# A four-layer graph network on one core: projections moved into layer 0's second pass over adj, and the sorting of rows moved beside layer 1's relayout

## The chip, the core and the metric

The kernel runs on one core of one Trainium2 chip. The metric is the device time in microseconds of one execution; lower is better. The kernel before takes 3336.72 us (median of three executions, 3329.15 to 3339.13).

## The reference

Four layers over N = 2708 nodes of 128 features, all with the same adjacency matrix `adj` (2708 x 2708, fp32, about five non-zeros a row, among them the diagonal). Each layer adds to x what it makes of the normed rows h = max(layernorm(x), 0). Layers 0 and 1 and their hand-over are what the change touches:

```python
# layer 0
fc = h @ W + b
d = sum(adj, axis=1); s = 1 / (sqrt(d) + 1e-8)
x = x + (adj * s[:, None] * s[None, :]) @ fc
# layer 1: h again from the new x; Wq, Wk, Wv are 1024 x 128
q, k, v = ((h @ Wi.T).reshape(128, N, 8) for Wi in (Wq, Wk, Wv))
a = softmax(einsum('dnh,dmh->dnm', q, k) / sqrt(128) + 2 * adj, axis=2)
x = x + einsum('dnm,dmh->dnh', a, v).reshape(N, 1024) @ Wo.T
# layer 2: adj.T @ h / degree, two projections, batch norm, relu
# layer 3: sigmoid gates between neighbours, weighted by adj
```

Layer 1 has 128 "heads" d, of 2708 nodes and 8 features each. A head takes its nodes from the reshape, so the projections' result has to be written to DRAM and read back in another order. The kernel evaluates exp of the small logits by a polynomial and corrects the few neighbours of a node by themselves; for this it needs the list of each row's non-zeros (column and value, up to 16), and it works on the rows sorted by their number of neighbours.

## The kernel before

The rows are cut into 22 tiles of 128 (the last has 20). In layers 0 and 1 the order of instructions on each engine is the program's own (`tc.manual_schedule()`): nothing reorders them, and what should lie side by side is written side by side, by generators that are advanced step by step.

**Start (lines 254 to 350).** All of x is loaded; the three weights of layer 1 are loaded and turned (`by_head`); the first three tiles of adj are asked for. All 22 tiles are normed: statistics on VectorE (326, 327), root (329), scaling on VectorE (338), relu on ScalarE (342), transposes in groups of four (344) into `hT` (345). Then fc per tile, two matmuls, the second with one row for the bias (348, 349), and a copy (350).

**First load (386 to 417).** Each adj tile passes once, in an order that alternates between the `STAY` = 8 tiles that stay in SBUF, transposed, and the others. ScalarE sums the rows (393) and takes the root (397); VectorE finishes the scale factor (398, 399) and scales fc (400). For the ten tiles in `early` (0 to 7, 8 and 9) the search for neighbours is done too. Tiles that stay are transposed (`turned`, 303, copies 308), and products of staying tiles with fc tiles already scaled are issued a few at a time (`products`, 363). At the end `x` is updated for the eight (414).

**Search for neighbours (129 to 176).** Five generator steps per tile: the 8 largest of each of five segments (134); their places (138); the 16 largest of the 40 (144 to 148, with casts on GpSimd, 155 to 157); a one-hot of 16 x 40 on VectorE (160), multiplied by the columns on GpSimd (166); a sum over 40 on VectorE (174). `look(n)` advances it.

**Second load (493 to 522).** The other 14 tiles are loaded again (`rows_of_adj`, four buffers, asked for three tiles ahead), searched, transposed, tested for negative values on ScalarE (488, 506) and multiplied with all fc tiles (`product`, 469); `added` (476) updates x. When four tiles are done, their norm for layer 1 is queued and advanced two steps per tile (`norm`).

**Projections (620 to 655).** For each group of 512 rows (148 in the last) 24 matmuls (641), one per weight and head feature, six PSUM banks; each is written to one of 25 columns of `qkv`, by ScalarE and VectorE in turn (648, 650), so to a stride of 100 bytes; the group is stored to `qkv_c` (652). Between them `in_order` is advanced: it ranks the rows by number of neighbours (a prefix sum on VectorE) and scatters their lists into `list_d` with 22 indirect DMAs on GpSimd's queue (612).

**Layer 1 (686 to 1369).** `prepare` loads a group of four heads (`raw`, 548) and squares it (796). The main loop goes through 128 heads in six chunks each; GpSimd makes most of the keys' features and the value products two heads ahead (1150, `keys`, `with_values`). Beside it a chain of generators is advanced 1.5 steps per chunk: `by_node` (relayout of q, k, v from heads to nodes through DRAM, 195 steps), then `sorted_rows` (loads `list_d`), then `from_neighbours`.

Of the kernel before, what the change touches and what calls it, by code (L numbers as in the profile page):

```python
# [28 lines left out]
STAY = 8  # L29
# [16 lines left out]
def gnn4_kernel(  # L46
# [82 lines left out]
    def neighbours(t, sz, a, pool, seg0, at48):  # L129
# [41 lines left out]
        )  # L171
        yield
        col = pool.tile([P, KS], FP, name="n_col")
        nc.vector.reduce_sum(col[:sz], hot[:sz], axis=AX.X)
# [80 lines left out]
    pre = ExitStack()  # L255
    bp = pre.enter_context(tc.tile_pool(name="l01", bufs=1))
    hT = bp.tile([C, N], FP, name="hT")
    with ExitStack() as ph:
        lp = ph.enter_context(tc.tile_pool(name="l0", bufs=1))
        hp = ph.enter_context(tc.tile_pool(name="l0_h", bufs=3))  # L260
        np_ = ph.enter_context(tc.tile_pool(name="l0_n", bufs=2))
# [4 lines left out]
        pa = ph.enter_context(tc.tile_pool(name="l0_pa", bufs=1, space=PSUM))  # L266

        def by_head(src, name):

            nat = ap.tile([P, KC, C], FP, name=f"{name}_nat", tag="a_nat")  # L270
            nc.sync.dma_start(nat, src.rearrange("(t p) c -> p t c", p=P))
            dst = bp.tile([P, HEAD, C], FP, name=name)
            for i0, iw in _cuts(KC, 4):
                pt = ps.tile([P, BK], FP, name="w_ps", tag="tr")
                for i in range(iw):
                    nc.tensor.transpose(pt[:, i * P : (i + 1) * P], nat[:, i0 + i], ident)
                c0, cw = i0 * P // HEAD, iw * P // HEAD
                nc.vector.tensor_copy(
                    dst[:, :, c0 : c0 + cw],
                    pt[:, : iw * P].rearrange("p (c h) -> p h c", h=HEAD),  # L280
                )
            return dst
# [5 lines left out]
        def rows_of_adj(t):  # L288
            r0, sz = rows[t]
            a = ap.tile([P, N], FP, name="a_nat", tag="a_nat")  # L290
            nc.sync.dma_start(a[:sz], adj[r0 : r0 + sz])
            return a

        def turned(t, a, both):

            sz = rows[t][1]
            at = tp.tile([P, NT, P], FP, name="a_tr")
# [16 lines left out]
        fc = lp.tile([P, NT, C], FP, name="fc")  # L314
        junk = lp.tile([P, N], BF, name="junk")
        mv = lp.tile([P, NT, 2], FP, name="mv_0")
        nc.gpsimd.memset(mv, 1.0)
        with tc.manual_schedule():
            stay, gone = list(range(STAY)), list(range(STAY, NT))
            order = [t for two in zip(stay, gone) for t in two] + gone[STAY:]  # L320
            early = stay + gone[:2]
            wT = [by_head(w, f"wT{i}") for i, w in enumerate((wq, wk, wv))]
            nat = [rows_of_adj(t) for t in order[:3]]
            for t, (_, sz) in enumerate(rows):
                st = hp.tile([P, nc.vector.BN_STATS_DIM], FP, name="ln_st")
                nc.vector.bn_stats(st[:sz], x_sb[:sz, t])
                nc.vector.bn_aggr(mv[:sz, t], st[:sz])
            rstd = lp.tile([P, NT], FP, name="rstd_0")
            nc.scalar.activation(rstd, mv[:, :, 1], AF.Sqrt, bias=eps)
            nc.vector.reciprocal(rstd, rstd)  # L330
            for t0, tw in _cuts(NT, 4):
# [3 lines left out]
                for t in range(t0, t0 + tw):  # L335
                    sz = rows[t][1]
                    h = hp.tile([P, C], FP, name="h_0", bufs=4)
                    nc.vector.tensor_scalar(
                        h[:sz], x_sb[:sz, t], mv[:sz, t, 0:1], rstd[:sz, t : t + 1],
                        ALU.subtract, ALU.mult,  # L340
                    )
                    nc.scalar.activation(h[:sz], h[:sz], AF.Relu)
                    o = (t - t0) * P
                    nc.tensor.transpose(pt[:, o : o + sz], h[:sz], ident[:sz, :sz])
                nc.scalar.copy(hT[:, s0 : s0 + w], pt[:, :w])
            for t, (r0, sz) in enumerate(rows):
                pf = pm.tile([P, C], FP, name="fc_ps", tag="mm")
                nc.tensor.matmul(pf[:sz], hT[:, r0 : r0 + sz], w0_sb, start=True, stop=False)
                nc.tensor.matmul(pf[:sz], ones[0:1, :sz], b0_sb, start=False, stop=True)
                nc.scalar.copy(fc[:sz, t], pf[:sz])  # L350

            sums0 = [pa.tile([P, 4, C], FP, name=f"l0_s{g}") for g in range(-(-STAY // 4))]
# [18 lines left out]
            seg_i = lp.tile([P, SEG, 8], I32, name="seg_i")  # L371
            nc.gpsimd.iota(seg_i, pattern=[[seg_w, SEG], [0, 8]], base=0, channel_multiplier=0)
            seg0 = lp.tile([P, CAND], FP, name="seg0")
            nc.gpsimd.tensor_copy(seg0, seg_i.rearrange("p s e -> p (s e)"))
            at_i = lp.tile([P, CAND], I32, name="at_i")
            nc.gpsimd.iota(at_i, pattern=[[1, CAND]], base=0, channel_multiplier=0)
            at48 = lp.tile([P, CAND], FP, name="at48")
            nc.gpsimd.tensor_copy(at48, at_i)
            found = []

            def look(n):
                for _ in range(n):
                    while found and next(found[0], "done") == "done":
                        found.pop(0)

            seen = []
            for i, t in enumerate(order):
                r0, sz = rows[t]
                if i + 3 < NT:
                    nat.append(rows_of_adj(order[i + 3]))  # L390
                a = nat[i]
                look(3)
                nc.scalar.activation(
                    junk[:sz], a[:sz], AF.Copy, accum_out=deg[:sz, t : t + 1]
                )
                d = dinv[:sz, t : t + 1]
                nc.scalar.activation(d, deg[:sz, t : t + 1], AF.Sqrt)
                nc.vector.tensor_scalar_add(d, d, 1e-8)
                nc.vector.reciprocal(d, d)
                nc.vector.tensor_scalar_mul(fc[:sz, t], fc[:sz, t], d)  # L400
# [5 lines left out]
                products(8 if t in stay else 14)  # L406
                seen.append(t)
                ready += [(j, t) for j in sorted(there)]
                ready += [(t, m) for m in seen[:-1] if t in stay]
            look(6)  # L410
            nat = [rows_of_adj(t) for t in gone[:3]]
            products(len(ready))
# [6 lines left out]
            rs1 = lp.tile([P, NT], FP, name="rs1")  # L419
            normed = []  # L420

            def normed_rows(t0, tw):

                hg = hp.tile([P, 4, C], FP, name="h_1", bufs=2)
                for t in range(t0, t0 + tw):
                    sz = rows[t][1]
                    st = hp.tile([P, nc.vector.BN_STATS_DIM], FP, name="ln_st")
                    nc.vector.bn_stats(st[:sz], x_sb[:sz, t])
                    nc.vector.bn_aggr(mv[:sz, t], st[:sz])
                yield  # L430
                r = rs1[:, t0 : t0 + tw]
                nc.scalar.activation(r, mv[:, t0 : t0 + tw, 1], AF.Sqrt, bias=eps)
                yield
                nc.vector.reciprocal(r, r)
                for t in range(t0, t0 + tw):
                    sz = rows[t][1]
                    nc.vector.tensor_scalar(
                        hg[:sz, t - t0], x_sb[:sz, t], mv[:sz, t, 0:1], rs1[:sz, t : t + 1],
                        ALU.subtract, ALU.mult,
                    )  # L440
                for t in range(t0, t0 + tw):
                    sz = rows[t][1]
                    nc.scalar.activation(hg[:sz, t - t0], hg[:sz, t - t0], AF.Relu)
                yield
                pt = ps.tile([P, BK], FP, name="ln_ps", tag="tr")
                s0 = rows[t0][0]
                w = rows[t0 + tw - 1][0] + rows[t0 + tw - 1][1] - s0
                for t in range(t0, t0 + tw):
                    sz = rows[t][1]
                    o = (t - t0) * P  # L450
                    nc.tensor.transpose(pt[:, o : o + sz], hg[:sz, t - t0], ident[:sz, :sz])
                nc.scalar.copy(hT[:, s0 : s0 + w], pt[:, :w])
                yield

            def norm(n):
                for _ in range(n):
                    while normed and next(normed[0], "done") == "done":
                        normed.pop(0)

            groups = _cuts(NT, 4)  # L460
            while groups and sum(groups[0]) <= STAY:
                normed.append(normed_rows(*groups.pop(0)))
# [11 lines left out]
            def added(t, po):  # L474
# [5 lines left out]
                if groups and sum(groups[0]) == t + 1:  # L480
                    normed.append(normed_rows(*groups.pop(0)))
# [13 lines left out]
            for t in range(STAY, NT):  # L495
                if t + 3 < NT:
                    nat.append(rows_of_adj(t + 3))
                a = nat[t - STAY]
                sz = rows[t][1]
                if t not in early:  # L500
                    found.append(neighbours(t, sz, a, np_, seg0, at48))
                    look(2)
                there[t] = turned(t, a, False)
                if t - STAY + 1 < STAY:
# [4 lines left out]
                )  # L509
                if t > STAY:  # L510
                    pos[t - 1] = product(t - 1)
                if t - 2 in pos:
                    added(t - 2, pos.pop(t - 2))
                look(3)
                norm(2)
# [5 lines left out]
            while normed:  # L521
                norm(1)

    VW = HEAD + 1
    QKV = 3 * HEAD + 1
# [1244 lines left out]
```

## Time and profile before

| | us |
|---|---|
| median of three executions (3329.15 to 3339.13) | 3336.72 |
| the profiled execution, of its own | 3354.19 |
| its span | 3352.4 |
| start, norm, fc | 0 to 70 |
| first load | 70 to 211 |
| second load | 211 to 379 |
| projections, last matmul | 379 to 494 |
| last projections in DRAM | 511 |
| first square of layer 1 (796) | 540 |
| relayout's last copy | 931 |
| layer 1's last weighted moments (1210) | 2814 |

The profile names instructions by line, engine and operation, with the tiles that they write and read. A group's row gives its busy time, the mean of one instruction, and the idle time just before with what ended it. A table of stretches gives for each window its length, the busy time of PE (matmul), PEld (weight load), DVE (VectorE), ACT (ScalarE) and POOL (GpSimd) with the number of instructions, the granted TensorE clock, the share of the DMA engines and GB/s. A line of waits reads: engine, tile and line that waited, what it waited for, time in total, times, longest.

### The profile page before, as it was taken

The numbers are of one execution on the slowest core, as the hardware profiler recorded it, in microseconds if no ns is written. First come the engines' busy times: TensorE is split into PE (matmuls) and PEld (weight loads), VectorE is DVE, ScalarE is ACT, GpSimd is POOL, SyncE is SP. The second block draws the span as 40 slices with busy tenths as digits, with TensorE's granted clock in tenths as the row PEclk, the third lists the DMA queues.
The fourth block names the chain that finished last, engine by engine and source line by source line (L and its number), as shares of the span: only waits on it lengthen the run. The fifth ranks groups of instructions, "written<-read, shape, count | busy, mean of one in ns | idle before, by whom it ended". The sixth has DMA issues, their size and how long they took to land. (4 is left out here: it accounts for less than half of the span.)

```text
span 3352.4 us, 50866 instructions
## 1 busy us (share of the span) xinstructions
PE 2691.7 (80%) x17781; PEld 2273.0 (68%) x17781; DVE 2202.7 (66%) x5135; ACT 1314.8 (39%) x3127; POOL 2009.3 (60%) x2263
## 2 busy tenths in 40 slices
PE   6477884888789999999999999999888897796044
PEld 4476543777788887888888788877777886443033
DVE  3868753666678888888888788887666675213222
ACT  3485462555544444444444444444322232102010
POOL 0111115555588888888988888889656663000775
PEclk6688896999999999999999999999888999895565
DMA  3452274777743333333334333343465712541322
GB/s 113 175 227 93 76 326 128 208 214 206 211 131 114 125 125 127 128 132 128 119 138 139 126 141 125 137 143 121 94 148 143 166 48 64 193 176 56 106 83 61
DMA packets 312741, 462.08 MB, mean 138 GB/s; under 512 B 159650, under 2 KB 234404, under 8 KB 289330
## 3 DMA queue, kind: packets, MB, share of 16 engines
q1 hardware_dynamic: 280870, 289.79, 28.3%
q0 software_dynamic: 31600, 168.86, 14.7%
q8 instruction: 148, 2.42, 0.3%
q14 instruction: 123, 1.01, 0.1%
HBM read 344.89 MB, written 113.67 MB: 137 GB/s over the span
## 5 line engine op out<-in xcount | busy, mean ns | idle before, releaser
L1238 PE MATMUL g_ps<-mw,fT 128*128 128x128 f32 x5632 | 817.5, 287 | 155.2 <-ACT fT L1228 115.1
L1238 PEld LDWEIGHTS g_ps<-mw,fT 128*128 128x128 f32 x5632 | 715.4, 196 | 290.6 <-ACT fT L1228 178.4
L1228 ACT COPY fT<-f_ps 128x512 f32<-128x512 f32 (+1 forms) x768 | 420.6, 548 | 1216.7 <-PE f_ps L1226 1216.6
L1200 PE MATMUL m_ps<-y,fk 128*128 128x128 f32 (+1 forms) x5632 | 768.2, 280 | 0.0
L1200 PEld LDWEIGHTS m_ps<-y,fk 128*128 128x128 f32 (+1 forms) x5632 | 699.9, 194 | 15.4
L1150 POOL TENSOR_TENSOR y<-bk,raw 128x792 f32<-128x792 f32 x256 | 415.8, 1624 | 432.1 <-ACT y L1181 420.3
L1246 DVE TENSOR_TENSOR z<-g_ps,bq 128x324 f32<-128x324 f32 (+1 forms) x768 | 355.6, 463 | 435.0 <-PE g_ps L1238 433.6
L1226 PE MATMUL f_ps<-ident,fq 128*128 128x128 f32 x2816 | 441.6, 276 | 14.4 <-DVE v_sum L817 9.3
L1252 DVE TENSOR_REDUCE o_raw<-z 128x36 f32<-128x324 f32 (+1 forms) x768 | 355.8, 463 | 26.4
L1150 POOL TENSOR_TENSOR fk<-bk,raw 128x352 f32<-128x352 f32 (+1 forms) x384 | 357.7, 955 | 0.1
L1226 PEld LDWEIGHTS f_ps<-ident,fq 128*128 128x128 f32 x2816 | 340.2, 144 | 16.2 <-DVE v_sum L817 10.6
L1150 POOL TENSOR_TENSOR fk<-raw,bk 128x352 f32<-128x352 f32 (+1 forms) x512 | 312.6, 640 | 3.1 <-ACT bk L719 2.3
L1147 DVE TENSOR_TENSOR fq<-bq,kq_ps 128x528 f32<-128x528 f32 (+1 forms) x512 | 288.2, 605 | 0.0
L930 POOL TENSOR_TENSOR c_z<-c_kv,c_q 128x1024 f32<-128x1024 f32 (+1 forms) x121 | 284.2, 2349 | 2.2 <-DMA c_kv<-kv_n,srt 1.4
L971 PE MATMUL v_ps<-c_v,ident 128*128 128x512 f32 (+1 forms) x484 | 233.3, 605 | 15.3 <-ACT c_acc L986 15.3
L1591 POOL DMA_INDIRECT g<-gate_d,srt x121 | 120.4, 995 | 110.2 <-issue 109.0
L1147 DVE TENSOR_TENSOR fq<-kq_ps,bq 128x352 f32<-128x352 f32 (+1 forms) x512 | 171.9, 378 | 0.0
L155 POOL CAST n_fl<-n_ci 128x40 f32<-128x40 int32 (+1 forms) x22 | 4.8, 218 | 251.9 <-DVE n_ci L138 251.9
L936 DVE TENSOR_REDUCE c_c<-c_z 128x128 f32<-128x1024 f32 (+1 forms) x121 | 147.5, 1219 | 3.4 <-POOL c_z L930 3.2
L954 DVE TENSOR_TENSOR c_v<-c_kv,c_c 128x1024 f32<-128x1024 f32 (+1 forms) x121 | 146.7, 1212 | 0.0
L971 PEld LDWEIGHTS v_ps<-c_v,ident 128*128 128x128 f32 (+1 forms) x484 | 82.0, 189 | 79.1 <-issue 58.8
L915 POOL DMA_INDIRECT c_kv<-kv_n,srt x121 | 117.8, 974 | 23.1 <-issue 9.6
(290 smaller groups left out, 3714.1 us busy)
## 6 DMA issues: line engine op xcount, KB each, us to landing
a_nat<-in_adj_dram SPq DMA_DIRECT2D x34, 1354.0 KB
qkv_c<-qkv SPq DMA_DIRECT2D x5, 6400.0 KB
a<-in_adj_dram SPq DMA_DIRECT2D x21, 1354.0 KB
kv_n<-n_kv SPq DMA_DIRECT2D x16, 1344.0 KB
o_g<-o_raw SPq DMA_DIRECT2D x32, 396.0 KB
q_n<-n_q SPq DMA_DIRECT2D x16, 672.0 KB
o_cr<-o_c SPq DMA_DIRECT2D x21, 512.0 KB
r_raw<-o_g SPq DMA_DIRECT2D x22, 396.0 KB
```

What stands on the lines that cost most here:

```text
L930: nc.gpsimd.tensor_tensor(zs[b][:sz], kvs[b][:sz, 0, :, 0], qs[t][:sz], ALU.mult)
L936: nc.vector.reduce_sum(cs[b][:sz], zs.pop(b)[:sz], axis=AX.X)
L954: nc.vector.tensor_tensor(z[:sz], kv[:sz, 0, :, 1].rearrange("p (j c) k -> p j c k", j=2), c.rearrange("p (j c) -> p j c", j=2)[:, :, :, None]
L971: nc.tensor.matmul(accs[t][:sz, j], ident[:sz, :sz], z[:sz, j].rearrange("p c k -> p (c k)"), start=s0 == 0, stop=s0 == ROOM[t] - 1,)
L1147: nc.vector.tensor_tensor(o, x, y, ALU.mult)
L1150: nc.gpsimd.tensor_tensor(o, x, y, ALU.mult)
L1200: nc.tensor.matmul(pms[d][:, :P], fks[d][:sz, t], ys[d, h][:sz, m * VW * B_ALL : m * VW * B_ALL + P], start=t == 0, stop=t == NT - 1,)
L1226: nc.tensor.transpose(pt[:, m], fqs[d][:, t0 + m], ident)
L1228: nc.scalar.copy(fts[d, c][:, :n], pt[:, :n])
L1238: nc.tensor.matmul(pg[:, m], ft[:, m], mws[d], start=True, stop=True,)
L1246: nc.vector.tensor_tensor(z[:, :n], pg[:, :n, : B_ALL * VW].rearrange("p t (k b) -> p t k b", k=VW), bqs[d % 2][:, t0 : t0 + n, None, :B_A ...
L1252: nc.vector.reduce_sum(ros[g][:, t0 : t0 + n, i], z[:, :n], axis=AX.X,)
```

## The change

Layer 0 keeps six tiles in place of eight. The first two adj tiles are asked for ahead of the weights; their row sums (and tile 0's transposes and first search steps) are issued between the groups of the first norm, ahead of the weights' transposes and of fc. The norm's scaling goes from VectorE to GpSimd, its relu is one instruction per group, fc's copies are one per four tiles, and the scaling of fc goes to ScalarE. Adj tiles are asked for four ahead, behind a tile's work. The ten early searches are tiles 0 to 5, 13, 15, 17, 19, so every second tile in the order. The search's sum over 40 is begun on GpSimd (40 to 20 to 10 to 5) and ended on VectorE.

In the second load the norm of layer 1 is queued in groups of two tiles, each followed by the projections of its two tiles: 24 matmuls of 128 columns a tile, four to a PSUM bank (three banks), written four adjacent floats at a time by ScalarE and VectorE in turn, and a store per tile. This flow is advanced 11 steps per tile, at five places of the loop. What is left of it is run after the loop. The separate phase of projections is gone.

`in_order` becomes the last thing beside `by_node` in layer 1: each step of the relayout advances it by one, with two steps per scatter.

```diff
-STAY = 8
+STAY = 6
...
+        w = CAND
+        while w % 2 == 0:
+            w //= 2
+            nc.gpsimd.tensor_tensor(
+                hot[:sz, :, :w], hot[:sz, :, :w], hot[:sz, :, w : 2 * w], ALU.add
+            )
         yield
         col = pool.tile([P, KS], FP, name="n_col")
-        nc.vector.reduce_sum(col[:sz], hot[:sz], axis=AX.X)
+        nc.vector.reduce_sum(col[:sz], hot[:sz, :, :w], axis=AX.X)
...
+        op = ph.enter_context(tc.tile_pool(name="l0_qkv", bufs=1))
...
-        pa = ph.enter_context(tc.tile_pool(name="l0_pa", bufs=1, space=PSUM))
+        pa = ph.enter_context(tc.tile_pool(name="l0_pa", bufs=3, space=PSUM))
...
-            early = stay + gone[:2]
-            wT = [by_head(w, f"wT{i}") for i, w in enumerate((wq, wk, wv))]
-            nat = [rows_of_adj(t) for t in order[:3]]
+            early = stay + gone[STAY + 1 :: 2][:4]
+            nat = {t: rows_of_adj(t) for t in order[:2]}
+            w_nat = []
+            for i, w in enumerate((wq, wk, wv)):
+                w_nat.append(tp.tile([P, KC, C], FP, name="w_nat", tag="a_tr"))
+                nc.sync.dma_start(w_nat[i], w.rearrange("(t p) c -> p t c", p=P))
+            for t in order[2:4]:
+                nat[t] = rows_of_adj(t)
+            ots = [op.tile([P, P, QKV], FP, name=f"qkv{i}") for i in range(2)]
+            for ot in ots:
+                nc.gpsimd.memset(ot[:, :, 3 * HEAD :], 1.0)
...
+            def scaled(t0, tw):
+
+                hg = hp.tile([P, 4, C], FP, name="h_g", bufs=2)
+                for t in range(t0, t0 + tw):
+                    sz = rows[t][1]
+                    nc.gpsimd.tensor_scalar(
+                        hg[:sz, t - t0], x_sb[:sz, t], mv[:sz, t, 0:1], rs1[:sz, t : t + 1],
+                        ALU.subtract, ALU.mult,
+                    )
+                whole = sum(rows[t][1] == P for t in range(t0, t0 + tw))
+                if whole:
+                    nc.scalar.activation(hg[:, :whole], hg[:, :whole], AF.Relu)
...
+            def front(i, last):
+
+                t = order[i]
+                sz = rows[t][1]
+                a = nat.pop(t)
                 look(3)
+                if last is not None:
+                    d = dinv[: rows[last][1], last : last + 1]
+                    nc.vector.tensor_scalar_add(d, d, 1e-8)
+                    nc.vector.reciprocal(d, d)
                 nc.scalar.activation(
                     junk[:sz], a[:sz], AF.Copy, accum_out=deg[:sz, t : t + 1]
                 )
...
+                nc.scalar.activation(dinv[:sz, t : t + 1], deg[:sz, t : t + 1], AF.Sqrt)
+                if last is not None:
+                    f = fc[: rows[last][1], last]
+                    nc.scalar.activation(f, f, AF.Copy, scale=d)
                 if t in early:
                     found.append(neighbours(t, sz, a, np_, seg0, at48))
                     look(2)
                 if t in stay:
                     there[t] = turned(t, a, False)
...
+                if i + 4 < NT:
+                    nat[order[i + 4]] = rows_of_adj(order[i + 4])
...
+            stats(0, NT)
+            spread(0, NT)
+            for n, (t0, tw) in enumerate(_cuts(NT, 4)):
+                turned_rows(t0, tw, scaled(t0, tw))
+                if n in (1, 3):
+                    front(n // 2, None)
+            wT = [by_head(n, f"wT{i}") for i, n in enumerate(w_nat)]
...
+            for i in range(2, NT):
+                front(i, order[i - 1])
+                back(order[i - 1])
+                products(6 if order[i] in stay else 9)
...
+            def projected(t):
+
+                r0, sz = rows[t]
+                ot = ots[t % 2]
+                for i in range(3):
+                    for e0 in range(0, HEAD, 4):
+                        pq = pa.tile([P, 4, P], FP, name="qkv_ps", tag="s")
+                        for e in range(4):
+                            nc.tensor.matmul(
+                                pq[:, e, :sz], wT[i][:, e0 + e], hT[:, r0 : r0 + sz],
+                                start=True, stop=True,
+                            )
+                        yield
+                        scale = (C**-0.5, 1.0, 1.0)[i]
+                        to = ot[:, :sz, i * HEAD + e0 : i * HEAD + e0 + 4]
+                        src = pq[:, :, :sz].rearrange("p e r -> p r e")
+                        turns[0] += 1
+                        if turns[0] % 2:
+                            nc.scalar.mul(to, src, scale)
+                        else:
+                            nc.vector.tensor_scalar_mul(to, src, scale)
+                nc.sync.dma_start(qkv_c[:, r0 : r0 + sz], ot[:, :sz])
+                yield
+
+            def row_group(t0, tw):
+
+                stats(t0, tw)
+                yield
+                spread(t0, tw)
+                yield
+                hg = scaled(t0, tw)
+                yield
+                turned_rows(t0, tw, hg)
+                yield
...
+                    yield from projected(t)
...
-            groups = _cuts(NT, 4)
+            groups = _cuts(NT, 2)
...
                 if t not in early:
                     found.append(neighbours(t, sz, a, np_, seg0, at48))
                     look(2)
+                go(1)
                 there[t] = turned(t, a, False)
+                go(2)
                 if t - STAY + 1 < STAY:
                     positive(t - STAY + 1)
...
+                if t + 4 < NT:
+                    nat[t + 4] = rows_of_adj(t + 4)
+                go(3)
                 if t > STAY:
                     pos[t - 1] = product(t - 1)
+                go(2)
                 if t - 2 in pos:
                     added(t - 2, pos.pop(t - 2))
                 look(3)
-                norm(2)
+                go(3)
...
+        def in_order():
...
+                nc.gpsimd.indirect_dma_start(
+                    out=list_d,
+                    out_offset=bass.IndirectOffsetOnAxis(ap=at[:sz, t : t + 1], axis=0),
+                    in_=rec[:sz, t],
+                    in_offset=None,
+                )
+                yield
+                yield
+
+        def side_by_side(a, b):
+
+            for _ in a:
+                next(b, None)
+                yield
+            yield from b
...
-        first = chain(by_node(), sorted_rows(), from_neighbours())
+        first = chain(side_by_side(by_node(), in_order()), sorted_rows(), from_neighbours())
```

## The prediction

> **What bounds the kernel now.** I cut the span into its stages, then read what each stage waits for. The table of stretches (length, then busy time of PE, PEld, DVE, ACT, POOL) gives start and norm, first load, second load, projections, hand-over to layer 1:
>
> ```profile
> 0.00:67.00 67.00, 39.41 (x126) 27.75 (x126) 18.32 (x73) 14.55 (x49) 4.71 (x40) 0.63 0.37 128
> 67.00:214.00 147.00, 88.58 (x559) 82.25 (x558) 108.16 (x339) 87.02 (x133) 23.80 (x50) 0.72 0.53 200
> 214.00:379.00 165.00, 123.84 (x928) 113.74 (x926) 129.88 (x393) 101.92 (x184) 28.66 (x61) 0.86 0.24 86
> 379.00:497.00 118.00, 114.12 (x293) 53.52 (x292) 79.31 (x103) 73.18 (x73) 17.10 (x19) 0.97 0.60 253
> 497.00:552.00 55.00, 4.00 (x14) 2.94 (x14) 8.59 (x35) 4.12 (x12) 16.93 (x26) 0.51 0.62 208
> ```
>
> Both loads are near DVE's limit (108 of 147 and 130 of 165 us); projections are PE's (114 of 118); in the hand-over all engines idle. DVE's timeline in the first load shows one row's search for neighbours after the other:
>
> ```profile
> 73.51 3.21 DVE L134 MAX8 n_cv<-a_nat 128x8 f32<-128x542 f32 x5
> ...
> 84.19 0.82 DVE L174 TENSOR_REDUCE n_col<-n_hot 128x16 f32<-128x640 f32 x1 [1.73 <-POOL n_hot L166]
> ...
> 85.51 3.21 DVE L134 MAX8 n_cv<-a_nat 128x8 f32<-128x542 f32 x5
> ```
>
> A search takes 12.0 us, 1.73 of them a wait for POOL. PE's timeline of the second load shows what a row costs PE where nothing holds it: 22 products 5.2 us, 22 transposes 2.6 us:
>
> ```profile
> 291.29 5.27 PE L469 MATMUL l_o<-fc,a_tr 128*128 128x128 f32 x44
> 296.49 2.75 PE L303 MATMUL a_ps<-ident,a_nat 128*128 128x128 f32 x22
> ```
>
> The waits between 494 and 560 us name what ends the hand-over:
>
> ```profile
> POOL list_d L612 <- DMA list_d<-rec,s_at: 34.7, 6, 8.5
> DVE W L780 <- DMA list_d<-rec,s_at: 28.6, 1, 28.6
> DVE w_r L767 <- DMA qkv_c<-qkv: 16.1, 1, 16.1
> ```
>
> Layer 1's first tiles wait 16.1 us for the last projections to land and 28.6 us more for the sorting's scatters (each waits for the one before).
>
> [...] around 313 to 324 us PE stood 10.97 us between two transposes because ACT, whose copies it needed, stood behind a square root waiting for DVE. My whole second-load sum rests on it. [...] 512 elements to a stride of 100 bytes took 1.10 us on DVE, 512 contiguous ones 0.69. [...] The scatters here start at least 2.42 us apart (0.96 issue, 1.46 wait).
>
> **Part 1, norm and first load.** Two of 22 adj tiles are fronted between the norm's groups, and 10 searches (as before) are spread over every second tile. DVE's statistics start near 8.5 us instead of 16 (x lands before the first weights, which were used at 10.5): 22 x 0.40 = 8.7, root with table load 1.6, so the norm's groups start at 19.3. Six groups on ACT at about 2.0 us each, the two sums 2 x 2.85, tile 0's copies 3.3 and PE's turns among them end near 44; the weights' 24 transposes near 48.5. Then the 44 fc matmuls with their one-row bias, 31.5 us in the trace (38.4 to 69.9), the same instructions: 80. ACT stands behind them. In that time DVE finishes two searches, then waits for tile 1's sum until 83.7, and starts its third at 90.5. A search is now: 11.42 as measured without the three small operations (73.51 to 84.93), less 0.6 (the reduction shrinks from 640 to 80 elements), plus POOL's adds of 320, 160, 80 elements. On POOL 640 took 1.54, 352 0.85, 88 0.43, 40 0.27, so 0.8 + 0.5 + 0.4, overlapped: 1.5 (1.2 to 1.8). They lie in a wait, because the three steps follow each other without other DVE work. 12.3, with two tiles' scale factors 0.76: 13.1. 90.5 + 8 x 13.1 = 195; last products, six additions to x: 200, against 210.8. **-11** (-25 to 0). POOL's scaling replaces 22 DVE operations of 0.34; POOL isn't shown doing it; 0.3 to 0.5 each, hidden behind ACT's 2.0 per group. fc's scaling (0.29) goes to ACT, which waits for DVE in that stage anyway; at worst 20 x 0.29 = 6. The qkv tiles' memsets come early on an idle POOL: nothing.
>
> **Part 2, second load with projections.** Work per row on PE: 2.6 + 5.2, and of 528 projections with 128 columns (in place of 144 with 512) four make a group. Four 128-wide matmuls take 0.89 to 1.06 us in layer 1: 0.97. 132 groups are 128 us against 114 before. Steps run 11 a row, of 18 per two tiles (4 norm, 12 groups, 2 stores): 7.3 groups a row. PE 7.8 + 7.1 + 0.3 = 15.2. Evictions write four contiguous floats: between 0.59 and 1.12 on ACT, 0.69 and 1.10 on DVE; I take 0.65 and 0.75[...]. DVE for a row with search: 12.3 + 3.7 x 0.75 + 0.9 = 15.9.
>
> If the queues ran freely, the bound would be 15 to 16 us a row. They don't. Three PSUM banks; a group needs the eviction of the group three before, every second of which is DVE's; DVE's eviction is queued behind the search's first half (6.65 us, row start) or second (5.85 with its hand-overs, after the products), and its search's second half behind an eviction that waits for PE. I followed the queues by hand through rows 6 to 12. Row 10: search 87.2 to 93.8 (clock from the stage's start), PE's fourth bank free at 94.6, two more groups to 97.5, products to 102.8, group to 103.7, its DVE eviction to 104.5, addition, second half to 110.6, eviction and statistics to 112.1: 25 us. In row 11 ACT's root waits for those statistics, and its tile copies for the root. Row 8 takes 22, row 9 19, row 12 17.6: rows 6 to 12 end at 155. Rows 14, 16, 18, 20 at 22 are 88, the searchless 13, 15, 17, 19 at 17.5 are 70, row 21 18: 331. After the last row come 33 steps (24 groups, six of them narrow: 21) with two norm chains (6): 27. Stage 358, against 283.5 (210.8 to 494.3): **+75** (-12 to +110). The two rows moved here by STAY are in it. ACT is no bound: 16 x (2.9 copies + 2.65 test) + 6 x 3.0 + 66 x 0.65 + 11 x 1.0 = 161. SP's queue gets 22 stores of 1.6 MB ahead of adj loads that are four rows early[...].
>
> **Part 3, hand-over.** The last store is 20 rows behind 128, not 148 behind 512: landing 6 us after the last projection instead of 16.4: **-10** (-12 to -6). The scatters' 28.6 us go. What is late next is the load of raw: issued from 511.1, one group is 1.1 MB, at the stretch's 208 GB/s 5.4 us[...]: 519 for the first square instead of 539.7: **-20** (-27 to -12).
>
> **Part 4, sorting beside the relayout.** 22 scatters of 1 us enter POOL's queue, two steps apart: 1.33 of the loop's 2.84 us chunks (130 chunks to 933 us). Each waits for its forerunner, and keys and value products of the next heads are queued behind. The wait was 1.46 with quiet DMA, about 5 while raw was loading, 8 to 9 under the big stores; with DMA busy 0.75 here, 4.2. In a head of 17 us POOL has 9.4 of work and 4.5 scatters: 4.5 x 5.2 = 23.4. Over 4.9 heads the excess is 31; POOL's lead of 7 us and the 8 us of relayout stalls (ACT waited 31.7 us for q_n over the stage) cover half: 16. The sort's 11 us of DVE and two matmuls in the single bank of the transposes: 4. **+20** (0 to +80).
>
> **The sum.** -11 + 75 - 10 - 20 + 20 = +54. The profiled execution is 3354.2 (span 3352.4), 17.5 above the median of the runs shown; I carry the difference to the median: 3336.7 + 54 = 3391.
>
> **Rivals.** *Free queues, faster:* engines overlap in the second load. PE-bound: 16 x 15.2 + 27 = 270, so -13; DVE-bound 12 x 15.9 + 4 x 15.2 + 27 = 279, so -5. The sum is -34 to -26, **3307**. For it: before, DVE kept its pace beside PE (12.6 a row). Against: there, neither waited for the other inside a row. It decides below 17.3 us a row, where the stage is 304 and all gains and losses cancel. *Break-even:* rows near 17.5: **3337**. *POOL decides:* waits of 8 us per scatter: 4.9 x 4.5 x 9 = 198 against 83 normal, +100 for part 4 with the cover gone: **3455**. Against: layer 1's writes are small, not the projections' 6.4 MB. That the sorting only moves its wait is part of this.
>
> **Chances.** Forecast 0.48; free queues 0.27; break-even 0.11; POOL 0.14. 0.3% of the time (10 us) is about what a measurement can tell from none. Faster 0.28, same 0.10, slower 0.62. The range leaves out the ends of the first and last: 3300 to 3445.
>
> **What would show it.** Start of the second load's first search near 200; last projection near 558; PE idle in that stage before projections, released by DVE and ACT evictions; the first square some 14 us after it (before: 45); POOL waiting for list_d in layer 1 some 20 times. I am wrong if rows take under 17.3 us, if evictions cost 1.1, or if layer 1 from its first square to its end keeps its length.

## The result, and the profile after

| | us |
|---|---|
| before, median of four executions (3329.15 to 3339.13) | 3334.96 |
| after, median of four executions (3388.54 to 3392.42) | 3389.65 |
| ratio, 95% interval | 1.0166, 1.0149 to 1.0184 |
| after, the profiled execution, of its own | 3392.42 |
| its span | 3390.6 |

The changed kernel is slower by 54.7 us. The stages of both profiled executions, each from one event that both kernels have to the next:

| stage | before | after | difference | forecast |
|---|---|---|---|---|
| start to the first update of x (414, then 496) | 210.8 | 202.3 | -8.5 | -11 |
| second load and projections, to the last projection's matmul | 283.1 | 351.0 | +67.9 | +75 |
| hand-over, to the first weighted moments (1210, then 1265) | 68.7 | 30.7 | -38.0 | -30 |
| relayout, to its last copy (855, then 841) | 368.8 | 404.5 | +35.7 | +20 |
| rest of layer 1, to the last weighted moments | 1883.0 | 1888.7 | +5.7 | 0 |
| the tail behind it, which the change doesn't touch | 538.0 | 513.4 | -24.6 | 0 |

The tail is the profile's, not the change's: in all other kernels of this study it takes 509 to 517 us, so the profiled execution of before was unlucky there by some 23 us. Without the tail the differences sum to +62.8; before's profiled execution with a tail of 515 would be 3331, 4 below its median, and after's is 3 above: 62.8 - 7 = 56, which agrees with the medians.

The table of stretches of the changed kernel (start and norm, first load, second load with projections, hand-over, relayout; busy time of PE, PEld, DVE, ACT, POOL, then the granted clock, the DMA share and GB/s):

```profile
0.00:70.00 70.00, 35.94 (x140) 26.60 (x140) 30.09 (x107) 18.37 (x32) 30.30 (x81) 0.79 0.47 163
70.00:203.00 133.00, 74.92 (x396) 68.51 (x396) 75.56 (x251) 79.18 (x124) 32.53 (x64) 0.67 0.53 200
203.00:554.00 351.00, 276.62 (x2137) 262.61 (x2135) 162.66 (x466) 149.82 (x264) 65.87 (x118) 0.87 0.39 149
554.00:584.00 30.00, 9.97 (x58) 8.99 (x58) 11.42 (x27) 6.19 (x18) 19.73 (x31) 0.57 0.64 181
584.00:990.00 406.00, 317.17 (x2409) 297.62 (x2410) 256.39 (x611) 205.50 (x458) 236.53 (x294) 0.90 0.67 182
```

In the third line no engine is full: TensorE, the busiest, stands for 74 of 351 us at a clock of 0.87. The waits of that stage say for what (engine, tile and line that waited, what for, us in total, times, longest):

```profile
DVE qkv L523 <- PE qkv_ps L511: 133.0, 44, 11.8
...
ACT qkv L521 <- PE qkv_ps L511: 100.1, 44, 7.6
...
PEld ln_ps L400 <- ACT h_g L387: 48.0, 8, 9.4
...
DVE n_col L180 <- POOL n_hot L175: 43.8, 12, 3.7
ACT rs L373 <- DVE mv L368: 39.7, 10, 13.5
ACT h_g L387 <- POOL h_g L381: 35.8, 11, 8.5
```

VectorE waits for TensorE (its evictions of projections, 133 us), ScalarE for VectorE's statistics, TensorE for ScalarE's relu: a circle. The timeline of the changed kernel shows one turn of it (start, duration, engine, line; in brackets the idle time before and what ended it), here VectorE, then ScalarE, then TensorE:

```profile
306.64 0.69 DVE L523 TENSOR_SCALAR qkv<-qkv_ps 128x512 f32<-128x512 f32 x1 [6.39 <-PE qkv_ps L511]
...
313.52 0.24 DVE L180 TENSOR_REDUCE n_col<-n_hot 128x16 f32<-128x80 f32 x1 [3.64 <-POOL n_hot L175]
...
314.27 0.28 DVE L367 BATCH_NORM_STATS2 ln_st<-x_sb 128x6 f32<-128x128 f32 x1
...
321.64 0.15 DVE L374 RECIPROCAL rs<-rs 128x2 f32<-128x2 f32 x1
...
315.20 0.29 ACT L373 ACTIVATE rs<-mv,eps 128x2 f32<-128x2 f32 x1 [6.99 <-DVE mv L368]
315.40 1.54 ACT L316 COPY a_tr<-a_ps 128x512 f32<-128x512 f32 x3
...
316.02 2.40 PE L311 MATMUL a_ps<-ident,a_nat 128*128 128x128 f32 x10 [6.32 <-ACT a_tr L316]
324.05 0.69 PE L400 MATMUL ln_ps<-ident,h_g 128*128 128x128 f32 x2 [5.63 <-ACT h_g L387]
```

VectorE is held 6.39 us by an eviction whose matmuls come late, then makes its search's second half (with 3.64 us for GpSimd), and only then the statistics (314.27). ScalarE's root has waited 6.99 us for them, with the copies of the transposes behind it, so TensorE stood 6.32 us. Next VectorE makes the following search's first half, and the reciprocal, which the norm needs, stands behind it until 321.64: TensorE stands again, 5.63 us, before the norm's transposes.

In the hand-over and the relayout of the changed kernel:

```profile
POOL bk L1195 <- DMA qkv_c<-qkv: 18.7, 1, 18.7
ACT sq L782 <- DMA raw<-qkv_c: 13.2, 1, 13.2
```

```profile
POOL list_d L911 <- DMA list_d<-rec,s_at: 42.6, 16, 6.1
...
POOL list_d L911 <- DVE s_at L908: 8.3, 1, 8.3
```

The 28.6 us for the scatters are gone from before layer 1 (first fence), and GpSimd pays 42.6 us for them inside it (second fence, from the waits of the relayout alone).

### The profile page after: what moved, and what is told of

Its sections match the earlier page's. It is cut to its first block, busy times and chain, and to the rows that moved or that the text cites. A ratio compares the mean times of both kernels' runs of the same rounds, so it can differ in the third digit from the quotient of the medians.

```text
span 3390.6 us, 52472 instructions
## 1 busy us (share of the span) xinstructions
PE 2730.2 (81%) x18549; PEld 2366.5 (70%) x18549; DVE 2150.9 (63%) x5068; ACT 1284.2 (38%) x3109; POOL 2077.0 (61%) x2373
## 5 line engine op out<-in xcount | busy, mean ns | idle before, releaser
L511 PE MATMUL qkv_ps<-hT,wT 128*128 128x128 f32 (+1 forms) x1056 | 144.1, 299 | 18.2 <-DVE qkv L523 8.7
L511 PEld LDWEIGHTS qkv_ps<-hT,wT 128*128 128x128 f32 x1056 | 137.8, 214 | 24.0 <-ACT hT L401 10.9
L1202 DVE TENSOR_TENSOR fk<-bk,kq_ps 128x528 f32<-128x528 f32 x128 | 89.5, 699 | 84.9 <-POOL bk L1205 84.8
```

Of the source, the lines that this page charges most:

```text
L511: nc.tensor.matmul(pq[:, e, :sz], wT[i][:, e0 + e], hT[:, r0 : r0 + sz], start=True, stop=True,)
L1202: nc.vector.tensor_tensor(o, x, y, ALU.mult)
```

## Experiments

Each is named by its kernel of origin. The time before was measured again beside each group: 3333.7 to 3336.0. Theory after the result: the second load loses by an interlock of engines, on each of which work stands behind a wait (6.39, 6.99 and 5.63 us in the turn above), and by its two more rows, the relayout by GpSimd's waits for its own scatters.

### Before, with six tiles kept

```diff
-STAY = 8
+STAY = 6
-            early = stay + gone[:2]
+            early = stay + gone[:4]
```

> The kernel before with one part of the change: six tiles of adj stay in place of eight (the ten early searches are kept at ten, tiles 0 to 9). Theory: the first load is paced by its ten searches of 12 us on VectorE, so taking two tiles' transposes and products out of it shortens it by less than 5 us, while the second load gets two more rows at the 12.0 us a row that it takes here (168 us for 14 rows): 24 - 4 = +20, 3355 us. Rival: the products only move from one load to the other and the sum of both stays: within 5 us, 3335 to 3340.

Measured: 3357.7, ratio 1.0070 (1.0051 to 1.0088): +22. The stretches of this kernel: first load, second load, projections.

```profile
70.00:215.00 145.00, 66.40 (x393) 61.28 (x393) 105.42 (x326) 78.36 (x110) 23.71 (x50) 0.68 0.49 185
215.00:399.00 184.00, 145.15 (x1086) 134.04 (x1084) 133.02 (x406) 109.63 (x202) 28.59 (x61) 0.88 0.30 107
399.00:514.00 115.00, 113.87 (x292) 53.49 (x292) 78.98 (x103) 72.83 (x73) 17.06 (x19) 0.97 0.60 253
```

The second load grows from 168 to 184, projections keep their 115, and the first load becomes not shorter but 4.6 longer (its update of x at 215.4). TensorE has 16 us less to do there, and nothing is gained by it; that the load even grew may come from the ten searches standing in the first eleven rows here, in place of fifteen, which this run doesn't separate. So the rival is out. The theory's total came out, but by other terms: the two rows cost 8 us each, not 12 (neither is searched), and the first load lost 5 us where 4 were to be gained.

### Before, with only the sorting moved

In the diffs of this section, code that is moved as in the change is not repeated.

```diff
-            sort = in_order(so, ps)
...
-        first = chain(by_node(), sorted_rows(), from_neighbours())
+        first = chain(side_by_side(by_node(), in_order()), sorted_rows(), from_neighbours())
```

> The kernel before with only the sorting moved beside layer 1's relayout, as in the change. As predicted on record: the hand-over loses 20 us of scatters and layer 1 gains 20, so 3335 us. Theory after the result: layer 1 gains 35 to 41 us from the 22 scatters alone, so -20 + 38 = +18, 3353. Rival: the longer layer 1 of the changed kernel comes from elsewhere (where its tiles lie, or the spread of its profile), the scatters cost nothing there: -20, 3315.

Measured: 3349.5, ratio 1.0037 (1.0029 to 1.0046): +14. The hand-over falls from 68.7 to 47.1 us, the relayout grows from 368.8 to 406.0, as in the changed kernel (404.5). So the longer relayout is the sorting's, all of it, and the recorded +20 for it was too small.

### After, with the projections last

```diff
-                for t in range(t0, t0 + tw):
-                    yield from projected(t)
+                late.extend(range(t0, t0 + tw))
...
+            for t in late:
+                for _ in projected(t):
+                    pass
```

> The changed kernel, but each tile's projections wait until the second load's loop is through; the norms stay in the loop, the matmuls stay 128 wide. Theory (interlock: evictions, search and norm queue behind each other): rows fall from 17.8 us to some 13.5, 16 of them 216 us; 132 groups at the 0.90 us that they take at the end of the stage are 119 us more; 335 in place of 351 us: -16, 3374. Rival (the mixture does hide work, rows are only as long as PE's work): 16 rows of 12 to 13 us with little less to save, and the 119 us come on top of about 250 us of loop: +20 or more, 3410.

Measured: 3365.4, ratio to before 1.0091 (1.0074 to 1.0109): 24 less than the changed kernel. Its second load and its projections:

```profile
202.00:397.00 195.00, 136.98 (x1081) 126.46 (x1080) 121.04 (x402) 109.08 (x197) 66.13 (x118) 0.85 0.26 90
397.00:519.00 122.00, 121.83 (x1061) 121.38 (x1061) 44.11 (x66) 43.36 (x68) 0.00 (x0) 0.98 0.68 284
```

As in the first experiment, the second load is counted up to the first projection, so with the last rows' norms. 317 us one after the other, 351 mixed: the mixture costs 34 us instead of hiding some of the 122. The rows take 11.8 us up to the last product, at 391, even less than the 13.5 expected. This and the first experiment split the stage's +68: 16 for two more rows (184 against 168), 11 for the second load with norm and search in their new form (195 against 184), 7 for narrow matmuls (122 against 115), 34 for the mixture itself. What of the mixture costs that, the next experiments try.

### After, with all evictions on ScalarE

```diff
-                        if turns[0] % 2:
+                        if True:
                             nc.scalar.mul(to, src, scale)
```

> The changed kernel with all 132 evictions of projections on ScalarE, none on VectorE, so that VectorE's search never stands behind a matmul. Theory (the interlock goes over VectorE, which waits 133 us for matmuls in this stage): search and statistics run ahead, norm chains come earlier, 25 us less (10 to 40), 3365. Rival 1 (the stalls are the norm chain's own latency over four engines, or PE's work): within 5 us, 3390. Rival 2 (ScalarE's queue becomes the bound: 44 us more on it, and transposes' copies behind evictions): +10 to +30, 3410.

Measured: 3367.9, ratio 1.0102 (1.0079 to 1.0125): 22 less than the changed kernel; the stage is 327.9 in place of 351.0, although ScalarE now works 188 us in it. VectorE no longer waits for projections, and the largest of its waits is for the norm's root. The waits of this kernel's stage:

```profile
DVE rs L374 <- ACT rs L373: 122.1, 10, 23.7
ACT qkv L521 <- PE qkv_ps L511: 84.0, 81, 8.4
...
PEld ln_ps L400 <- ACT h_g L387: 32.1, 8, 9.0
```

TensorE's wait for the norm falls from 48.0 to 32.1 without any edit of the norm: part of it was VectorE being held by evictions. What is left may be the norm's own chain, which the next experiment tries.

### After, with the norms as a flow of their own

```diff
-                for t in range(t0, t0 + tw):
-                    yield from projected(t)
+                flow.extend(projected(t) for t in range(t0, t0 + tw))
+                yield
...
-                flow.append(row_group(*groups.pop(0)))
+                normed.append(row_group(*groups.pop(0)))
...
+                norm(3)
                 go(3)
```

> The changed kernel with the norms of the second load as a flow of their own, three steps a row, ahead of the projections' flow (11 steps a row), so that a group's norm runs while the matmuls of the group before are issued. Theory (TensorE's longest waits in this stage, 46 to 48 us in 8, are the norm's chain over VectorE, ScalarE and GpSimd): most of it is covered, the stage falls from 351 to about 325 us: 3365. Rival (the chain's wait only hides one for evictions and search on VectorE, which comes next): within 6 us, 3390.

The projections now also have all eleven steps of a row for themselves. Measured: 3369.1, ratio 1.0107 (1.0090 to 1.0124): 21 less than the changed kernel; the stage is 329.5. In this kernel's waits, TensorE's wait for the norm has fallen to a third, and one for evictions has come up, but smaller:

```profile
PEld qkv_ps L511 <- ACT qkv L521: 26.1, 9, 5.2
...
PEld ln_ps L400 <- ACT h_g L387: 16.3, 7, 2.9
```

### After, without the adds on GpSimd

```diff
-        while w % 2 == 0:
+        while False:
```

> The changed kernel, with the search's sum over 40 columns wholly on VectorE as before. Theory (in the first load one search follows the other on VectorE, and each waits 3.64 us for GpSimd in place of 1.73): the pair of rows falls from 13.25 to about 12.0 us, -10 in the first load and some -5 in the second: 3375. Rival (the search's length decides nothing, other queues do): within 4 us, 3390.

Measured: 3369.3, ratio 1.0110 (1.0082 to 1.0139): 20 less than the changed kernel. Two searches in a row in the first load's timeline, of the changed kernel:

```profile
85.91 3.20 DVE L134 MAX8 n_cv<-a_nat 128x8 f32<-128x542 f32 x5
...
98.49 0.24 DVE L180 TENSOR_REDUCE n_col<-n_hot 128x16 f32<-128x80 f32 x1 [3.64 <-POOL n_hot L175]
99.15 3.20 DVE L134 MAX8 n_cv<-a_nat 128x8 f32<-128x542 f32 x5
```

and without the adds:

```profile
85.54 3.20 DVE L134 MAX8 n_cv<-a_nat 128x8 f32<-128x542 f32 x5
...
96.19 0.82 DVE L180 TENSOR_REDUCE n_col<-n_hot 128x16 f32<-128x640 f32 x1 [1.71 <-POOL n_hot L166]
97.43 3.20 DVE L134 MAX8 n_cv<-a_nat 128x8 f32<-128x542 f32 x5
```

The adds save VectorE 0.58 us of reduction and make it wait 1.93 us longer: 13.24 a search against 11.89. First load -11.6 (its end at 190.7), second load -11.3.

### After, with the scatters further apart

```diff
                     in_=rec[:sz, t],
                     in_offset=None,
                 )
-                yield
-                yield
+                for _ in range(8):
+                    yield
```

> The changed kernel with eight steps of the relayout between two scatters of the sorting in place of two, so some 15 us in place of 4. Theory (the scatters cost layer 1 by GpSimd's waits for the one before, 42.6 us in 16 waits): the waits go, the relayout's stage falls from 404.5 to about 375 us (before: 368.8): -30, 3360. Rival (the cost is the work itself: 22 issues of 1 us on GpSimd and the prefix sum on VectorE, in a stage without slack): -10 or less, 3380.

Measured: 3368.6, ratio 1.0112 (1.0095 to 1.0128): 21 less than the changed kernel. GpSimd's waits for `list_d`'s DMAs are gone altogether, and the relayout takes 384.1 in place of 404.5. That is between the two expectations: 20 us were the waits, and 15 above before's 368.8 remain without them.

### Before, with the sorting moved and its scatters apart

The edits of the second and the seventh experiment together.

> The kernel before with only the sorting moved beside the relayout, eight steps between two scatters. Theory: the hand-over stays 22 us shorter (as with two steps), and the relayout's stage is at most 10 us longer than before in place of 37: -12 to -20, 3320, faster than before. Rival (the work itself costs as much as the waits): 3340 to 3350.

Measured: 3324.7, ratio 0.9976 (0.9969 to 0.9984): 9 less than before. The hand-over is 47.4, the relayout 384.6, again 15.8 above before. The move gains, but less than expected, by that rest.

### Before, with only the scatters moved

```diff
         for t, (_, sz) in enumerate(rows):
-            nc.gpsimd.indirect_dma_start(
...
-            if t % 2:
-                yield
...
-        first = chain(by_node(), sorted_rows(), from_neighbours())
+        first = chain(side_by_side(by_node(), scattered()), sorted_rows(), from_neighbours())
```

`scattered` issues the same 22 scatters, eight steps apart; the ranking stays beside the projections.

> The kernel before, the ranking (prefix sum on VectorE, two matmuls) left beside the projections, and only the 22 scatters beside the relayout, eight steps apart. With the whole sorting moved so, the relayout's stage was 384.6 us, 15.8 above before. Theory (the rest is GpSimd's 22 issues of 1 us in a stage in which others wait for GpSimd's products): the stage stays at 380 or more, 3320. Rival (the rest is the ranking on VectorE and in the one PSUM bank of the transposes): the stage falls to about 372, 3312.

Measured: 3317.7, ratio 0.9944 (0.9925 to 0.9964); the relayout takes 370.6. My theory fell, and the rival came out: 22 issues of 1.0 us on GpSimd, spread out, cost the relayout under 2 us, and the rest of 14 is the ranking. (The stage ahead, second load with projections, is 2.5 shorter without the ranking in it, 280.1 against 282.6, so moving the ranking costs some 11 in all.) The starts of VectorE's weighted moments, one per head, show where. With the whole sorting moved:

```profile
538.01 0.24 DVE L1215 TENSOR_TENSOR mw<-m_ps,W 128x81 f32<-128x81 f32 x1 [5.97 <-PE m_ps L1205]
558.16 0.24 DVE L1215 TENSOR_TENSOR mw<-m_ps,W 128x81 f32<-128x81 f32 x1
579.20 0.23 DVE L1215 TENSOR_TENSOR mw<-m_ps,W 128x81 f32<-128x81 f32 x1
```

with the scatters alone:

```profile
541.58 0.24 DVE L1221 TENSOR_TENSOR mw<-m_ps,W 128x81 f32<-128x81 f32 x1 [6.61 <-PE m_ps L1211]
554.31 0.24 DVE L1221 TENSOR_TENSOR mw<-m_ps,W 128x81 f32<-128x81 f32 x1 [0.61 <-PE m_ps L1211]
569.47 0.24 DVE L1221 TENSOR_TENSOR mw<-m_ps,W 128x81 f32<-128x81 f32 x1 [0.42 <-PE m_ps L1211]
```

The two heads in which the ranking lies take 20.2 and 21.0 us in place of 12.7 and 15.2: 13.3 of the 14. In the 41 us of the first two, VectorE is busy 35.7; in the 27.9 of the second two, 20.3. So its slack is nearly used up there. TensorE, too, stood 4.4 us at the ranking's first matmul, which waits for VectorE; what the matmuls cost and what VectorE's work costs wasn't tried apart.

### After, with four edits

Evictions on ScalarE, norms as a flow of their own, no adds, scatters apart.

> The changed kernel with the four edits together: all evictions of projections on ScalarE, scatters eight steps apart, the search's sum wholly on VectorE, norms as a flow of their own. Theory (evictions, search and norm chain are one interlock, so their gains in the second load overlap; first load and relayout add up): -12 first load, -20 relayout, -40 in the second load (351 to about 310; the three edits alone gave -23, -21 and -11): 3317. If the three are independent: -55 there, 3302. If ScalarE, with some 194 us of work, becomes the bound: 325 us there, 3335.

Measured: 3298.9, ratio 0.9892 (0.9872 to 0.9911): 37 less than before, 91 less than the changed kernel. First load -12.5, relayout -20.5, second load 285.0 in place of 351.0: -66.0, more than the three edits gave one by one (23.1 + 21.5 + 11.3 = 55.9). I had expected less than the sum, so it was wrong that "their gains in the second load overlap". The stretch of this kernel's second load:

```profile
190.00:475.00 285.00, 256.04 (x2140) 244.27 (x2138) 128.37 (x402) 185.84 (x329) 45.84 (x82) 0.96 0.49 184
```

The same number of matmuls takes TensorE 256.0 us in place of 276.6, at a clock of 0.96 in place of 0.87; in the kernels with one edit (evictions, norms, no adds) it took 274.1, 271.9 and 274.2 (clock 0.89, 0.91, 0.88). So the stage in which TensorE stood least (29.0 us, against 74.4 in the changed kernel) had the highest granted clock. Within the changed kernel's turn shown above it differed too: 26 matmuls ahead of the gaps (292.7 to 295.4) took 2.70 us at a granted clock of 1.00, and 24 behind them (325.2 to 330.3) took 5.10 us at 0.50. That the gaps are the cause wasn't tried apart. This kernel still has the ranking beside the relayout (384.1 us, against 370.6 with the scatters alone); no run puts the two together.

### After, projections last, no adds, scatters apart

The edits of the third, sixth and seventh experiment together.

> The changed kernel with projections after the loop, scatters eight steps apart and the search's sum wholly on VectorE. Theory: 3365 as with projections last alone, -20 relayout, -12 first load, -10 in a second load paced by its searches: 3323. It says whether, with the interlock mended, the mixture (the kernel of the four edits) hides anything: by the theory it hides little, some 6 us; a rival that holds the mixture to be worth its place wants 20 or more between them.

Measured: 3316.1, ratio 0.9946 (0.9927 to 0.9965). The stage is 306.6 against 285.0 of the mended mixture, the whole 17 us longer. So the expectation "it hides little, some 6 us" was too low: mended, the mixture is worth 17 to 22 us, where unmended it cost 34.

### Before, with the new front and the sorting

Eight tiles and the wide projections as before; norm with first tiles of adj as in the change, without the adds; sorting as in the eighth experiment.

```diff
-STAY = 6
+STAY = 8
...
-                products(6 if order[i] in stay else 9)
+                products(8 if order[i] in stay else 14)
```

(against the kernel of the experiment ahead of this one; the early searches are tiles 0 to 7, 17 and 19, and the phase of projections of before, not repeated here, replaces its own)

> The kernel before (eight tiles stay, projections 512 wide as a phase of their own) with two parts of the change: the norm with its first tiles of adj, without the adds on GpSimd, and the sorting beside the relayout, eight steps between scatters. Theory: 3325 as measured with the sorting alone, and the first load ends 20 us sooner (190.7 us as with the changed kernel without the adds, against 210.5): 3305, 30 below before. Rival (with eight tiles kept, TensorE's products in the first load fill what the search leaves, and it ends near 200): 3315.

Measured: 3316.1, ratio 0.9937 (0.9918 to 0.9956). The first load ends at 195.1, between theory and rival, and the second load with projections takes 292.0, 9 more than before, which neither had: so that the rival's time came out is chance. Up to the first projection the second load takes 180 us in place of 168, though the adds are gone; with projections last it was 195 in place of 184. So its new form (norms two tiles at a time and scaled by GpSimd, loads four ahead) costs 11 to 12 us in both; which part of it does wasn't tried. With projections as a phase of their own, eight tiles stay 17 us behind the kernel with four edits; eight tiles with the mended mixture wasn't tried.

## Why the prediction was right, point by point

The forecast of 3391 was met at 3389.65. The mechanism that carried it, VectorE, ScalarE and TensorE holding each other in the second load, is shown by the experiments that remove it. But that the sum came within 2 us is luck: hand-over and second load were 15 us better than forecast, layer 1 with the sorting 21 us worse, the start 2.5 worse. By stages that is +62.8 for a forecast of +54, and the rest of the gap lies between the profiled executions and their medians (7 us, as said with the table).

**Norm and first load, -11.** Measured -8.5, by the steps given: the norm's groups ended near 44, fc at 76 (forecast 80), a pair of rows took 13.25 (forecast 13.1). One term was too low: GpSimd's scaling takes 0.79 us each, not the 0.3 to 0.5 that were my estimate beside VectorE's 0.34; it was hidden in the first norm. What the forecast didn't see is that this part has 12 us to spare: it priced the adds at a search of 12.3 against 12.0 and left it at that, where 11.89 is to be had by leaving them out.

**Second load, +75.** Measured +68. Evictions took 0.69 and 0.67 (forecast 0.75 and 0.65, my estimates between the times of contiguous and of strided writes). Rows 6 to 12 were to take 155 us; from the test for negative values (593) of row 6 to that of row 13 it was 155.3 (216.9 to 372.2), from first transpose to first transpose 165 (203.1 to 368.4). Row by row the forecast was poorer: by the tests row 8 took 16.9 (forecast 22), row 12 took 27.7 (17.6). Row 11 is the turn shown above, and there the root waits for the statistics and the copies for the root, as was said. The later rows were shorter (16.1 us each from there to row 21, forecast 17.5 to 22), and what follows the last search was longer, 37 us in place of 27: two norm chains lie bare there. That STAY's two rows are in it was said without a size; they are 16 of the 68.

**Hand-over, -30.** Measured -38: landing 2.8 us behind the last projection in place of 16.4 (-13.6, forecast -10), from landing to the first square 9.0 in place of 29.0 (-20, as forecast; the forecast's 519 lies 2.5 us behind 511.1 and the load's 5.4, which was my estimate and not shown by itself), and from the square to the first weighted moments 18.6 in place of 22.9 (-4.3), where the forecast had nothing.

**Sorting beside the relayout, +20.** This step failed in size. "The sort's 11 us of DVE and two matmuls in the single bank of the transposes: 4" is 14 (the last of the single moves). The scatters' 16 are 20 to 21. The last 5.7, in layer 1 behind the relayout, are within what the profiles of this study differ by there (1883 to 1896). The ranking was mis-sized twice: summed over the timeline it takes VectorE some 18 us here, not the 11 to 12 that it took beside the projections, and VectorE had too little slack in these heads to hide it. I looked at GpSimd, which issues the scatters, and took VectorE's share for small.

**The rivals.** "Free queues" was priced at 3307, with 15.2 us a row and a stage of 270 to 279. It is what the change could have been: with evictions off VectorE, norms ahead and without the adds the stage is 285, and with the scatters apart too the kernel takes 3299. "POOL decides" didn't happen: a scatter waited 2.7 us on average (42.6 in 16), at most 6.1, not 8. Its price was also mis-summed: 3336.7 - 11 + 75 - 10 - 20 + 100 is 3471, not 3455.

## What to carry to other kernels

Work that was mixed into a loop to fill an engine's gaps didn't pay here while its instructions stood, in their engine's program order, between a producer and the engine that was to be filled (in the turn above ScalarE's copies stood behind a root that waited 6.99 us, and TensorE stood 6.32 us for them). Before mixing, list for each engine what stands behind each wait, and try the evictions on the engine on which the least that is urgent stands behind them. The same mixture cost 34 us with evictions on two engines and norms in the projections' flow, and gained some 20 with the evictions on one engine, the norms ahead and the adds gone. A chain of dependent DMAs may be hidden beside other work if its members are issued further apart than one takes to land (here 15.0 us apart on average, with 2.4 to 6.9 to land, in the kernel before with only the scatters moved, where GpSimd waited for none); the arithmetic that comes with it has to be priced on its own engine.

## What the runs showed of the hardware

In the kernel before with the sorting moved and its scatters apart, three of the ranking's nine adds on VectorE took 1.96, 1.22 and 1.14 us while GpSimd worked, in place of 0.52, 0.51 and 0.47 beside the projections in the kernel before. The first of them in the timeline, VectorE and GpSimd:

```profile
559.75 0.53 DVE L847 TENSOR_TENSOR s_two<-s_two 128x366 f32<-128x366 f32 x1
...
560.40 1.96 DVE L847 TENSOR_TENSOR s_two<-s_two 128x358 f32<-128x358 f32 x1
...
560.35 1.63 POOL L1155 TENSOR_TENSOR y<-bk,raw 128x792 f32<-128x792 f32 x1 [6.06 <-ACT y L1186]
```

The second add, of fewer elements, takes 1.96 us and ends 0.4 us after GpSimd's product that began just ahead of it. The three adds are longer by 2.8 us together, which is part of the 6.2 between the 17.9 us that the ranking takes VectorE there and the 11.7 beside the projections. That GpSimd's work is the cause wasn't tried apart.

GpSimd's subtract-and-multiply with two columns of scalars over 128 x 128 took 0.79 us in the changed kernel (median of 44), against 0.34 on VectorE in the kernel before (median of 22). The search's five maxima took 3.20 us for the tile of 20 rows as for one of 128, in the changed kernel.
